# Decoder kernel: places of the rotary, of the first projection, of a norm step and of the gates' transposes in the order of an attention loop

## The chip, the cores and the metric

One core of a Trainium2 chip runs the whole kernel in one launch. The metric is the device time of one execution in microseconds (us); lower is better. An execution is compared with others of the same kernel by its median over several runs.

## What is computed

Two decoder layers on `x` (32 batch rows of 100 tokens, width 256) with a context of 32 x 361 x 192. Each layer adds three parts to x in turn, each on a layer norm of x. Only two of the six parts run the loop that is changed:

- The first part of layer 0: causal self-attention of 16 heads (head width 16), without biases or rotary.
- The third part of layer 0: the same attention with rotary on what makes queries and keys, with biases, then a norm, a gate over 8 experts (softmax, best two) and the sum of the two experts' products, and a second norm.

```python
qkv = x @ w_qkv                                    # first part
scores = jnp.einsum('bhqd,bhkd->bhqk', q, k) / math.sqrt(HD)
scores = jnp.where(causal[None, None], scores, jnp.float32(-1000000000.0))
o = jnp.einsum('bhqk,bhkd->bhqd', jax.nn.softmax(scores, axis=-1), v)
...
q_in = _apply_rope(xh, sin, cos).reshape(B, S, E)  # third part: q and k from q_in, v from x
x1 = _layer_norm(x + attn_out, ln1_w, ln1_b)
gates = jax.nn.softmax(x1 @ gate_w.T + gate_b, axis=-1)
expert_outputs = jnp.einsum('bsd,efd->bsef', x1, expert_w) + expert_b[None, None]
```

All data is float32.

## The kernel before, in words

The six parts run one after the other as stages. x lies in SBUF as eight groups of four batch rows (G = 4, 400 tokens a group). `heads_attention` (from L275) serves the first and the third stage. It is handed functions for what differs: `norm(g, part)`, which makes the normed group g in four parts, `turn`, `res`, which adds the output to x, and `fill(s, part)`, which puts other work into the loop.

The loop (L461) has one step s for each batch row, 32 in all, and in the third stage nine more in which only fill works. It is written as a pipeline: in step s the scores of row s + 1 are made and masked, the weights of row s are transposed and summed with its values, and row s - 1 is divided and projected out. With i = s mod 4, the steps of a group also project queries and keys of the next group (m = 0 at i = 0, m = 1 at i = 1, both halves of the keys at i = 2) and norm the group after that. The order in which the code issues instructions is the order in which PE, DVE, ACT and POOL each run theirs (`in_order`): an instruction that waits holds up all behind it on its engine. Across engines, semaphores order what depends on each other.

The names that the text uses:

- `queries_or_keys(g, m)` (L289): two products into one PSUM tile, then copies. For m = 0, 1 there are two copies, one for even and one for odd heads. In the first stage ACT makes one (L309) and DVE the other (L311); in the third ACT makes both (L305). The keys are copied by ACT (L313, L315).
- `scores` (L348) writes two PSUM tiles sc, `masked` (L363) adds the mask on DVE, `lowered` (L372) takes the row maximum on DVE (L376) and subtracts it on POOL (L377), `exponentials` (L379) is on ACT (L382). Each is done in two halves of eight heads.
- `turn_weights` (L385): four times four transposes of exponentials on PE (L389) with a copy eT on ACT each (L394). The first two take the first half of the heads, the last two the second half.
- `values` (L327), `sums` (L398, with the copy `back` on ACT, L410), `divided` (L414: four transposes on PE, then reciprocal and product on DVE, L423 and L425), `turn_sums` (L428, copy oT on ACT, L437), `output` (L441).
- The tiles called mm share four PSUM banks between all of these; a new tile waits until the copy that empties its bank's last tile is done.
- In the first stage `norm` part 1 takes statistics (on DVE, with one power on POOL, L174), part 2 subtracts and scales on DVE (L183); parts 0 and 3 do nothing. `turn` transposes the group and copies it to xT (L210, L131, L133); it stays at the head of step i = 0.
- In the third stage `norm` part 0 takes statistics, part 1 scales on ACT (L192), part 2 transposes (L945), and part 3 makes the rotary xrT with four DVE instructions (L956, L958 twice, L961). `turn` only hands over.
- The third stage's `fill` (L1111 on): `gated` makes `xg`, expert inputs times gate, on DVE (L1061), in part 0 for the step's second expert and in part 3 for the next step's first; `experts` multiplies on PE in parts 1 and 2 (L1073) and adds to `acc` on DVE (L1079), from step 9 on. A table says at which 4 * i + part a group's `rows_of` (bias and norm after attention), `gating` (transposes of x1, product with the gate weights, softmax, best two) and `gates_turned` come, one group behind the attention.

Quoted from the loop before:

```python
if g < NG:
    if i == 0:
        turned_[g] = turn(g)
    for m in ((0,), (1,), (2, 3), ())[i]:
        queries_or_keys(g, m)
if i >= 1 and g + 1 < NG:
    norm(g + 1, i - 1)
```

Of the kernel before, what the change touches and what calls it, by code (L numbers as in the profile page):

```python
# [22 lines left out]
NG = B // G  # L23
# [43 lines left out]
def kernel(ctx: ExitStack, tc: tile.TileContext, io: dict, out: bass.AP):  # L67
# [19 lines left out]
    def sc_tile():  # L87
        return psum["sc"][1].tile([P, 2, 512], F32, tag="sc", name="sc")

    def mm_tile():  # L90
        return psum["mm"][1].tile([P, 512], F32, tag="mm", name="mm")
# [18 lines left out]
    def row(name, n=T):  # L110
        a, b = ROW_AT[name]
        return rows[:n, a:b]

    def col(name, i=0, n=P):
        a, _ = COL_AT[name]
        return cols[:n, a + i : a + i + 1]
# [10 lines left out]
    def evac(dst, src):  # L127

        turn[0] += 1
        if turn[0] % 2:  # L130
            nc.vector.tensor_copy(dst, src)  # L131
        else:
            nc.scalar.copy(dst, src)  # L133
# [67 lines left out]
    def transposed(dst, src, gain=None, bias=None, tiles=None):  # L201

        if tiles is None:
            ps = sc_tile()
            ps = [ps[:, 0, :], ps[:, 1, :]]
        else:
            ps = [tiles() for _ in range(2)]
        for c in range(2):
            for i in range(G):
                nc.tensor.transpose(  # L210
                    ps[c][:, i * T : (i + 1) * T], src[:, i, c * P : (c + 1) * P], ident[:T, :T]
                )
        for c in range(2):
            if gain is None:
                evac(dst[:, c, :], ps[c][:, :GT])
            else:
                evac_affine(dst[:, c, :], ps[c][:, :GT], col(gain, c), col(bias, c))
# [7 lines left out]
    def in_order(more=mybir.EngineType.Pool):  # L225

        e = mybir.EngineType
        return tc.manual_schedule(engines={e.PE, e.DVE, e.Activation, more})
# [46 lines left out]
    def heads_attention(pool, w, wo, bias, norm, turn, res, fill):  # L275
# [103 lines left out]
        def exponentials(s, hf):  # L379

            ex = pool.tile([T, 8, T], F32, tag="ex", name="ex", bufs=4)
            nc.scalar.activation(ex, sms.pop((s, hf)), AF.Exp, scale=0.25)  # L382
            exs[s, hf] = ex
# [63 lines left out]
        with in_order():  # L447
            for part in range(4):
                norm(0, part)
            turned_[0] = turn(0)  # L450
            for m in range(4):
                queries_or_keys(0, m)
            values(0)
            ps = scores(0)
            for hf in range(2):
                masked(0, hf, ps[hf])
                lowered(0, hf)
                exponentials(0, hf)
            for part in range(4):
                norm(1, part)  # L460
            for s in range(B + 1 + fill.steps):  # L461
                g, i = s // G + 1, s % G
                more = s + 1 < B
                if more:
                    ps = scores(s + 1)
                    masked(s + 1, 0, ps[0])
                if g < NG:
                    if i == 0:
                        turned_[g] = turn(g)
                    for m in ((0,), (1,), (2, 3), ())[i]:  # L470
                        queries_or_keys(g, m)
                if i >= 1 and g + 1 < NG:
                    norm(g + 1, i - 1)
                fill(s, 0)
                if 1 <= s <= B:
                    divided(s - 1)
                if more:
                    lowered(s + 1, 0)
                    masked(s + 1, 1, ps[1])
                if i == 3 and g + 1 < NG:  # L480
                    norm(g + 1, 3)
                if s < B:
                    turn_weights(s)
                fill(s, 1)
                if more:
                    lowered(s + 1, 1)
                    values(s + 1)
                if 1 <= s <= B:
                    turn_sums(s - 1)
                if more:  # L490
                    exponentials(s + 1, 0)
                if s < B:
                    sums(s)
                fill(s, 2)
                if 1 <= s <= B:
                    output(s - 1)
                if more:
                    exponentials(s + 1, 1)
                fill(s, 3)


# [10 lines left out]
    with tc.tile_pool(name="a0", bufs=2) as pool:  # L512
        xns = {}

        def norm(g, part):
            if part == 1:
                xns[g] = stats(xs[g], G, tag="n")
            elif part == 2:
                xn = pool.tile([T, G, D], F32, tag="xn", name="xn")
                centered(xn, xs[g], G, xns[g])  # L520
                xns[g] = xn
# [10 lines left out]
        def fill(s, part):  # L532
            pass
# [16 lines left out]
    with tc.tile_pool(name="x0", bufs=2) as pool, tc.tile_pool(name="x0p", bufs=1) as fixed:  # L550
# [288 lines left out]
        with in_order():  # L839
# [11 lines left out]
            for n in range(-4, B + 1):  # L851
# [14 lines left out]
                g = (n + 4) // G + 1  # L866
                if (n + 4) % G == 3 and g < NG:
                    lnTs[g] = latents_turned(lns.pop(g))
                g = (n + 5) // G
# [55 lines left out]
    with tc.tile_pool(name="f0", bufs=2) as pool:  # L925
# [44 lines left out]
        x1s, x1Ts, wts, accs = {}, {}, {}, {}  # L970

        parts = {}
# [15 lines left out]
        def gating(g, part):  # L988
            if part == 0:
                x1T = pool.tile([P, 2, GT], F32, tag="x1T", name="x1T")  # L990
                transposed(x1T, x1s.pop(g), "f0_ln1w", "f0_ln1b", tiles=mm_tile)

                pg = mm_tile()
                project(
                    pg[:, :GT], [f0_wg[:, c, :] for c in range(2)],
                    [x1T[:, c, :] for c in range(2)],
                )
                lgT = small.tile([E, GT], F32, tag="wtT", name="lgT", bufs=2)
                nc.scalar.activation(lgT, pg[:E, :GT], AF.Identity, bias=col("f0_gb", 0, E))
                x1Ts[g], parts[g] = x1T, lgT  # L1000
                return
            if part == 1:
                lgT = parts[g]
                pg = mm_tile()
                for i in range(G):
                    nc.tensor.transpose(
                        pg[:T, i * E : (i + 1) * E], lgT[:, i * T : (i + 1) * T], ident[:E, :E]
                    )
                lg = small.tile([T, G, E], F32, tag="lg", name="lg")
                p3 = pg[:T, : G * E].rearrange("p (g e) -> p g e", e=E)  # L1010
                nmx = small.tile([T, G], F32, tag="nmg", name="nmg")
                nc.vector.tensor_reduce(nmx, p3, AX.X, ALU.max, negate=True)
                nc.vector.tensor_tensor(lg, p3, bc(nmx, 2, E), ALU.add)
                nc.scalar.activation(lg, lg, AF.Exp)
                parts[g] = lg
                return
            lg = parts.pop(g)
            sm = small.tile([T, G], F32, tag="smg", name="smg")
            nc.vector.tensor_reduce(sm, lg, AX.X, ALU.add)
            nc.vector.reciprocal(sm, sm)  # L1020
            gt = small.tile([T, G, E], F32, tag="gt", name="gt")
            nc.vector.tensor_tensor(gt, lg, bc(sm, 2, E), ALU.mult)
            _, hot = top2(pool, gt, G, row("iota", P))
            wt = small.tile([T, G, E], F32, tag="wt", name="wt")
            nc.vector.tensor_tensor(wt, hot[:T, 0], hot[:T, 1], ALU.add)
            nc.vector.tensor_tensor(wt, wt, gt, ALU.mult)
            wts[g] = [wt]
# [83 lines left out]
        def fill(s, part):  # L1111

            g, i = s // G, s % G


            n = 2 * (s - 2 * G - 1)
            if part % 3 == 0:
                upto = n + part // 3 + 1
                if s >= B:
                    upto += 2  # L1120
                if s < B + G:
                    upto = min(upto, E * (NG - 1) - 1)
                while done[0] <= min(upto, loads[0] - 1):
                    gated(done[0])
                    done[0] += 1
                    gates()
            if 1 <= g <= NG:
                for at, f, *args in (
                    (3, rows_of, 0), (4, rows_of, 1), (6, rows_of, 2), (9, gating, 0),
                    (10, gating, 1), (11, gating, 2), (14, gates_turned),  # L1130
                ):
                    if 4 * i + part == at:
                        f(g - 1, *args)
                        if at == 14:
                            stored[0] = E * g
                            gates()
            if 3 <= g and i == 1 and part in (0, 1, 3):
                end(g - 3, part)
            if part in (1, 2) and 0 <= n < E * NG:
                experts(n // E, n % E // 2, part - 1)  # L1140
# [33 lines left out]
    with tc.tile_pool(name="a1", bufs=2) as pool, tc.tile_pool(name="a1p", bufs=1) as fixed:  # L1174
# [242 lines left out]
        with in_order():  # L1417
            for part in range(11):
                project_group(0, part)
            for n in range(16 * NG + 12):  # L1420
                g, at = n // 16, n % 16
# [501 lines left out]
    with tc.tile_pool(name="f1s", bufs=2, side="right") as pool, in_order(SP):  # L1923
# [134 lines left out]
        for n in range(len(units) + 2):  # L2058
            if n < len(units):
                h, m = units[n]  # L2060
# [243 lines left out]
```

## Time and profile before

| what | value |
|---|---|
| median of 3 runs (lowest, highest) | 3555.65 us (3551.82, 3564.07) |
| the profiled execution: time, span | 3556.24 us, 3554.4 us |
| mean granted TensorE clock | 0.975 |
| PE busy, share of the span | 3353.6 us, 94% |
| DVE, ACT, POOL busy | 1873.7 us (53%), 1602.8 us (45%), 1258.7 us (35%) |
| first stage's loop | about 36 to 282 us of the span |
| third stage's loop, with its start and tail | about 767 to 1345 us of the span |

PE is TensorE's matmul, PEld its weight load, DVE VectorE, ACT ScalarE, POOL GpSimd, SP SyncE. L12 is line 12 of the kernel. In the view of stages, each line is a stretch of the span (start:end in us), then its length, then busy us and instructions of each engine, the granted PE clock as a share of full speed, the busy share of DMA, and GB/s. In the view of waits, a line is: engine, what waited, `<-` who released it and with what, us in total, times, the longest. In the view in order of time, a line is: start, duration, engine, source line, operation, output `<-` inputs, sizes, count, and in brackets the idle time before it with its releaser. Several equal instructions in a row are merged, so a duration with x8 is that of all eight.

### The profile page before, as it was taken

The numbers are of one execution on the slowest core, as the hardware profiler recorded it, in microseconds if no ns is written. First come the engines' busy times: TensorE is split into PE (matmuls) and PEld (weight loads), VectorE is DVE, ScalarE is ACT, GpSimd is POOL, SyncE is SP. The second block draws the span as 40 slices with busy tenths as digits, with TensorE's granted clock in tenths as the row PEclk, the third lists the DMA queues.
The fourth block names the chain that finished last, engine by engine and source line by source line (L and its number), as shares of the span: only waits on it lengthen the run. The fifth ranks groups of instructions, "written<-read, shape, count | busy, mean of one in ns | idle before, by whom it ended". The sixth has DMA issues, their size and how long they took to land. (4 is left out here: it accounts for less than half of the span.)

```text
span 3554.4 us, 66360 instructions
## 1 busy us (share of the span) xinstructions
PE 3353.6 (94%) x25978; PEld 2256.7 (63%) x25978; DVE 1873.7 (53%) x5328; ACT 1602.8 (45%) x3533; POOL 1258.7 (35%) x917
## 2 busy tenths in 40 slices
PE   7998999978989987999999999999999999999997
PEld 5775666646556643333466666666666668899997
DVE  6777777747676755755456464554646542011111
ACT  4664666646444414567454454545444442211111
POOL 3445887744444421000233333333233332012221
PEclk9999999989999998999999999999999999999999
DMA  2002000000101111000100000000000003466665
GB/s 84 2 2 64 23 26 23 16 17 9 28 22 31 27 38 47 1 1 1 41 14 19 19 25 21 20 26 19 20 27 18 25 13 111 140 178 184 187 179 146
DMA packets 109218, 168.15 MB, mean 47 GB/s; under 512 B 14996, under 2 KB 89628, under 8 KB 108444
## 3 DMA queue, kind: packets, MB, share of 16 engines
q1 hardware_dynamic: 94238, 145.60, 13.5%
q0 software_dynamic: 12688, 15.36, 2.4%
q8 instruction: 207, 3.39, 0.4%
q10 hardware_dynamic: 1982, 2.95, 0.2%
q14 instruction: 103, 0.84, 0.1%
HBM read 138.32 MB, written 28.82 MB: 47 GB/s over the span
## 5 line engine op out<-in xcount | busy, mean ns | idle before, releaser
L1696 POOL TENSOR_TENSOR ex<-ex,rc 100x1444 f32<-100x1444 f32 x128 | 332.1, 2594 | 785.1 <-DVE rc L1695 743.4
L1687 ACT ACTIVATE ex<-s,nmx 100x361 f32<-100x361 f32 x512 | 303.1, 594 | 143.4 <-DVE nmx L1678 143.4
L377 POOL TENSOR_TENSOR s<-s,nmx 100x800 f32<-100x800 f32 x128 | 210.1, 1641 | 332.4 <-DVE nmx L376 251.1
L1294 ACT ACTIVATE h<-sc,cols 128x800 f32<-128x800 f32 x256 | 222.4, 924 | 134.1 <-PE sc L1288 133.7
L1678 DVE CUSTOM_DVE_ANT_0 s<-sc,mb 100x361 f32<-100x361 f32 x512 | 250.5, 527 | 7.6 <-PE sc L1671 7.6
L2151 POOL DMA_INDIRECT acc_dram<-y,xg x57 | 89.0, 1562 | 451.1 <-DVE y L2150 243.0
L2133 ACT ACTIVATE hgT<-sc 128x1024 f32<-128x1024 f32 x57 | 58.4, 1024 | 351.2 <-PE sc L223 344.8
L1073 PE MATMUL mm<-xg,f_we 128*128 128x400 f32 x512 | 195.2, 527 | 19.3 <-ACT back L410 11.2
L223 PE MATMUL sc<-xgT,w1b 128*128 128x128 f32 x1824 | 213.1, 275 | 0.4 <-DMA w1b<-in_f_w 0.4
L2150 DVE TENSOR_SCALAR y<-mm,gx 128x256 f32<-128x256 f32 x57 | 27.6, 484 | 348.1 <-PE mm L223 348.1
L223 PEld LDWEIGHTS sc<-xgT,w1b 128*128 128x128 f32 x1824 | 208.2, 192 | 0.7 <-issue 0.6
L223 PE MATMUL mm<-wx,hgT 128*128 x912 | 206.1, 379 | 0.0
L1671 PE MATMUL sc<-kT,qT 64*100 64x361 f32 x1024 | 197.6, 463 | 0.0
L1643 PE MATMUL mm<-x_wa,cT 128*128 128x512 f32 (+1 forms) x512 | 191.1, 496 | 0.1
L1703 PE MATMUL mm<-ident,ex 100*128 100x100 f32 (+1 forms) x1536 | 168.0, 257 | 18.7 <-ACT kT L1625 9.7
L223 PEld LDWEIGHTS mm<-wx,hgT 128*128 128x128 f32 x912 | 169.0, 190 | 20.6
L1721 PEld LDWEIGHTS mm<-eT,vb 128*64 128x64 f32 (+1 forms) x3072 | 136.7, 137 | 67.4 <-issue 66.2
L1613 PE MATMUL mm<-cT,x_wa 128*128 128x361 f32 x512 | 178.1, 471 | 0.7 <-DVE lnT L148 0.7
L174 POOL TENSOR_TENSOR rs<-va,neghalf 100x4 f32<-100x4 f32 (+1 forms) x96 | 95.4, 997 | 216.9 <-DVE va L170 120.4
L1703 PEld LDWEIGHTS mm<-ident,ex 100*128 100x128 f32 (+1 forms) x1536 | 142.6, 151 | 39.8 <-ACT kT L1625 14.0
L1710 ACT COPY eT<-mm 128x400 f32<-128x400 f32 (+1 forms) x256 | 125.7, 491 | 89.2 <-PE mm L1703 87.7
L1721 PE MATMUL mm<-eT,vb 128*64 128x100 f32 (+1 forms) x3072 | 162.3, 254 | 0.0
(346 smaller groups left out, 7221.6 us busy)
## 6 DMA issues: line engine op xcount, KB each, us to landing
w1b<-in_f_w SPq DMA_DIRECT2D x57, 1024.0 KB
wb<-wt_dram SPq DMA_DIRECT2D x64, 200.0 KB
wx<-in_f_w SPq DMA_DIRECT2D x8, 1024.0 KB
xg<-sorted_dram SPq DMA_DIRECT2D x57, 132.5 KB
cb<-in_ctx SPq DMA_DIRECT2D x32, 192.0 KB
cT<-in_ctxT SPq DMA_DIRECT2D x32, 180.5 KB
cT<-in_ctxT SPq DMA_DIRECT2D x64, 90.2 KB
x<-in_x SPq DMA_DIRECT2D x8, 400.0 KB
```

Of the source, the lines that this page charges most:

```text
L223: nc.tensor.matmul(ps, lhsT[k], rhs[k], start=(k == 0), stop=(k == n - 1))
L377: nc.gpsimd.tensor_tensor(sm, sm, bc(nmx, 2, T), ALU.add)
L1073: nc.tensor.matmul(ps[:, :GT], f0_we[:, k, e * D + m * P : e * D + (m + 1) * P], xgs[E * g + e][:, k, :], start=(i > 0 and e == 2 * i and ...
L1294: nc.scalar.activation(h1, both[r2][:, :, :GT], AF.Tanh, bias=col("a1_b1", o))
L1613: nc.tensor.matmul(kTs[u][c][:, :S2], x1_wa[:, m * P : (m + 1) * P], cT[:, 0, :], start=True, stop=False,)
L1643: nc.tensor.matmul(ps[e][:kn, :n], cT[:, 0, at], x1_wa[:, 1024 + c0 : 1024 + c0 + n], start=True, stop=False,)
L1671: nc.tensor.matmul(ps[:T, e, :S2], qT[p0 : p0 + 64, m, tok], kT[p0 : p0 + 64, c, :], start=True, stop=True,)
L1678: nc.vector.tensor_tensor_reduce(s[:, e, :], ps[:T, e, :S2], mb, 1.0, 3.4e38, ALU.add, ALU.min, nmx[:, e : e + 1],)
L1687: nc.scalar.activation(ex[:, 2 * c + e, :], s[:, e, :], AF.Exp, bias=nmx[:, e : e + 1], scale=-1.0, accum_out=sm[:, 2 * c + e : 2 * c + e ...
L1696: nc.gpsimd.tensor_tensor(ex, ex, bc(rc, 2, S2), ALU.mult)
L1703: nc.tensor.transpose(pt[:kn, j * T : (j + 1) * T], ex[:, j, k0 : k0 + kn], ident[:T, :T])
L1721: nc.tensor.matmul(po[64 * e : 64 * e + 64, m * T : (m + 1) * T], vb[k][:kn, v0 + 64 * h : v0 + 64 * h + 64] if k < 2 else vb[2 + u % 2][: ...
```

## The change

Five moves in the order of the code; no instruction is added or taken out, and no tile gets another size.

1. `queries_or_keys(g, 0)` at i = 0 is issued behind `turn_weights` and fill part 1, instead of right behind `turn`.
2. `norm(g + 1, 1)` at i = 2 is issued at that same place, instead of before `divided`.
3. `norm(g + 1, 3)` at i = 3 is issued at the end of the step, before fill part 3, instead of before `turn_weights`.
4. `gating` gets a fourth part: its transposes are a part of their own.
5. In fill's table the transposes go from place 9 to place 8 (i = 2, part 0, before `divided`); the gates' product stays at 9, and the two parts after it keep 10 and 11.

```diff
@@ heads_attention, the loop
                 if g < NG:
                     if i == 0:
                         turned_[g] = turn(g)
-                    for m in ((0,), (1,), (2, 3), ())[i]:
+                    for m in ((), (1,), (2, 3), ())[i]:
                         queries_or_keys(g, m)
-                if i >= 1 and g + 1 < NG:
+                if i in (1, 3) and g + 1 < NG:
                     norm(g + 1, i - 1)
                 fill(s, 0)
                 if 1 <= s <= B:
@@
                 if more:
                     lowered(s + 1, 0)
                     masked(s + 1, 1, ps[1])
-                if i == 3 and g + 1 < NG:
-                    norm(g + 1, 3)
                 if s < B:
                     turn_weights(s)
                 fill(s, 1)
+                if i == 0 and g < NG:
+                    queries_or_keys(g, 0)
+                if i == 2 and g + 1 < NG:
+                    norm(g + 1, 1)
                 if more:
                     lowered(s + 1, 1)
                     values(s + 1)
@@
                     output(s - 1)
                 if more:
                     exponentials(s + 1, 1)
+                if i == 3 and g + 1 < NG:
+                    norm(g + 1, 3)
                 fill(s, 3)
@@ gating
             if part == 0:
                 x1T = pool.tile([P, 2, GT], F32, tag="x1T", name="x1T")
                 transposed(x1T, x1s.pop(g), "f0_ln1w", "f0_ln1b", tiles=mm_tile)
+                x1Ts[g] = x1T
+                return
+            if part == 1:
+                x1T = x1Ts[g]
 
                 pg = mm_tile()
@@
-                x1Ts[g], parts[g] = x1T, lgT
+                parts[g] = lgT
                 return
-            if part == 1:
+            if part == 2:
                 lgT = parts[g]
@@ fill
-                    (3, rows_of, 0), (4, rows_of, 1), (6, rows_of, 2), (9, gating, 0),
-                    (10, gating, 1), (11, gating, 2), (14, gates_turned),
+                    (3, rows_of, 0), (4, rows_of, 1), (6, rows_of, 2), (8, gating, 0),
+                    (9, gating, 1), (10, gating, 2), (11, gating, 3), (14, gates_turned),
```

## The prediction

> **Reading order and what bounds the kernel.** I read the shares of the span first (PE 94% busy, DVE 53%, ACT 45%, POOL 35%), then busy time by stage, then who PE waits for in the two stages that the change touches, then the order of time of single steps there. "Step s" is one turn of the loop at L461, i = s mod 4; W1 to W4 are the four groups of `turn_weights`, D is `divided`, Q the projection of m = 0, X0 and X1 the expert products of fill parts 1 and 2.
>
> ```profile
> core 0: us, PE busy (x) PEld busy (x) DVE busy (x) ACT busy (x) POOL busy (x), PEclk, DMA share, GB/s
> 36.00:282.00 246.00, 233.25 (x3098) 173.14 (x3096) 182.34 (x331) 157.57 (x319) 104.22 (x131) 1.00 0.01 2
> 847.00:1267.00 420.00, 378.70 (x3225) 250.34 (x3224) 291.97 (x662) 179.97 (x358) 175.25 (x160) 0.98 0.11 28
> ```
> Only these stages run the edited loop (with the start, 767 to 847). The first leaves PE 13 us idle in 246, at full clock; the second 41 us in 420, and not always at full clock. In both PE sets the end, so an edit is worth the PE waits that it removes, less those that it makes. PE's waits from 847 to 1267:
>
> ```profile
> PE mm L1073 <- ACT back L410: 11.2, 4, 2.8
> PE mm L1073 <- DVE xg L1061: 8.1, 7, 1.9
> PE mm L210 <- ACT eT L394: 5.8, 5, 1.2
> PE mm L223 <- DVE x1T L148: 2.6, 4, 1.1
> PE mm L223 <- ACT x1T L139: 2.2, 3, 0.8
> ```
> The first and third to fifth are what the change aims at. How the first arises, in time (s = 15, i = 3):
>
> ```profile
> 993.04 4.07 POOL L377 TENSOR_TENSOR s<-s,nmx 100x800 f32<-100x800 f32 x1 [10.48 <-DVE nmx L376]
> 995.76 2.19 DVE L961 TENSOR_TENSOR xrT<-xrT,xwT 128x800 f32<-128x800 f32 x1
> 997.14 0.87 ACT L382 ACTIVATE ex<-s 100x800 f32<-100x800 f32 x1 [2.63 <-POOL s L377]
> 997.91 0.47 ACT L410 COPY back<-mm 128x400 f32<-128x400 f32 x1
> 998.44 5.70 PE L1073 MATMUL mm<-xg,f_we 128*128 128x400 f32 x8 [2.81 <-ACT back L410]
> ```
> POOL's `lowered` takes 4.07 us here and 1.52 elsewhere; the rotary's last add takes 2.19 instead of 0.98. They run at once and hold each other up. The exponential, the copy `back` behind it on ACT, and X1 (whose PSUM bank `back` frees) come late by that. X1 then takes 5.70 us instead of 2.95: PE fell to half clock.
>
> **Sum, first attention** (s = 0 to 31). No instruction is added anywhere; no DMA moves but the loads `wb`, which follow `xg` on SP.
>
> Q moved behind W: PE waits 0.88 us for `xT` between transposes and Q, six times in the trace (5.3 us), and W3 0.23 us for the bank that the qT copy frees. Now D and W1 (1.0 us of PE) cover the copies. W2 takes the bank of the first copy (done about 2.6 us after the scores start; W2 gets there at 2.8), so I see no new wait. On DVE the qT copy (0.64 us) now lies between the second mask and the second maximum; the weights need that result only in the next step, with some 2 us to spare. 6 x (0.88 + 0.23) = **-6.7 us**.
>
> `norm(g+1, 1)` at i = 2, here statistics on DVE (146.12 to 148.54, 2.4 us), moved behind the second mask:
>
> ```profile
> 148.47 0.26 DVE L423 RECIPROCAL rc<-mm 100x16 f32<-100x16 f32 x1
> 151.01 0.99 DVE L376 TENSOR_REDUCE nmx<-s 100x8 f32<-100x800 f32 x1
> 152.14 1.52 POOL L377 TENSOR_TENSOR s<-s,nmx 100x800 f32<-100x800 f32 x1 [0.40 <-DVE nmx L376]
> 153.69 0.88 ACT L382 ACTIVATE ex<-s 100x800 f32<-100x800 f32 x1 [0.67 <-POOL s L377]
> 154.06 1.70 PE L389 MATMUL mm<-ident,ex 100*100 100x100 f32 x16
> ```
> Where the statistics stand before, they are free: the reciprocal waits for D anyway, which PE ends at 148.4 behind two projections. Behind the second mask (ends 150.97) they push the second maximum to 153.3, its POOL add to 154.4 (the power of 1.02 us goes ahead of it on POOL, and is done by then), the exponential to 156.0 to 156.9. W3 of the next step reads it, and is due at 154.75: half of 1.70 us after 154.06, just after the exponential's present end at 154.57. So PE waits about 2.2 us, with W4, values, sums and output queued behind. ACT's four copies eT stand behind the same exponential, but W4 needs the first only at 157.4. Six groups: **+13.2 us**. Bounds: 0, if D came 2.4 us earlier (nothing moves it), and 2.4 each.
>
> Does such a hole also cost clock? The Trainium skill, page "TensorE: Matmul & The Clock Gate", section "Why this matters for your kernels", puts the limit at PE-idle gaps over about 3 us, a whole window of idle: 2.2 us would cost nothing. Stretches of 3.4 us of this trace say otherwise:
>
> ```profile
> 847.00:850.40 3.40, 1.50 (x33) 0.98 (x35) 3.23 (x12) 0.57 (x2) 1.78 (x5) 1.00 0.00 0
> 850.40:853.80 3.40, 3.40 (x44) 2.16 (x36) 2.48 (x4) 1.86 (x4) 3.00 (x3) 0.50 0.02 5
> ...
> 905.00:908.40 3.40, 2.17 (x22) 1.72 (x20) 2.34 (x5) 3.40 (x9) 1.52 (x1) 1.00 0.15 50
> 908.40:911.80 3.40, 2.65 (x8) 1.63 (x9) 0.67 (x1) 1.28 (x3) 0.00 (x0) 1.00 0.00 0
> ```
> PE busy 1.50 of 3.40 us (one gap of 1.90) gives half clock for the next 3.4; 2.17 does not. Of all such stretches in these stages none with over 55% busy is followed by half clock. So I take the trace: a gap of 2.0 us, of which 1.6 must fall in one stretch, trips in about two of three phases. Half clock for 3.4 us loses up to 1.7, I take 1.5: 4 x 1.5 = **+6 us** (by the rule 0; at most 6 x 1.7 = 10). The same page, section "Part 4: PE-mode transpose", says that transposes don't count as PE-busy in the same way. By that the new run of 28 transposes (xn, D, W, some 3 us) in front of Q would trip the clock at every i = 0: 6 x 1.7 = 10 us more. But the stretch at 905.00 holds transposes alone and keeps its clock; I count nothing.
>
> First stage: -6.7 + 13.2 + 6 = **+12.5 us**.
>
> **Sum, third stage.** Rotary (`norm(g+1, 3)`, 0.98 + 1.05 + 0.98 = 3.0 us of DVE uncontended) at the end of i = 3: POOL's add is back to 1.52 us and the exponential comes at 994.6. In the new order X1 also takes the bank of `turn_sums`, free since 994.5. X1 then follows the gates' product at 995.6. Gone: 4 x 2.81 = 11.2 us, and the half clock that the trace shows from 932.3, 997.2 and 1065.5 (3.4 + 6.8 + 3.4 us, half of it lost, 6.8). I take **-17 us**; bounds 11 and 18.
>
> Price, at i = 0 behind it (s = 12, 16, 20, 24): DVE starts the rotary only after `res` (0.5 us after the scores start), then come `xg`, the mask, the second `xg`. The first `xg` lands at 4.4, the second at 6.2; X0 is ready for them at 3.0 and 5.8, since Q no longer runs ahead of it. PE waits 1.4 + 0.4, with Q, values, sums and X1 behind, and saves 0.4 of old waits: 4 x 1.45 = +5.8, and about 1.2 for a clock that trips now and then: **+7 us**; bounds 0 and 13.
>
> Steps 0, 4, 8 have no experts: Q waits for the rotary (2.0, 1.6) or `back` (1.25), then W3 for Q's copies (1.8, 1.45), with a half-clock stretch at 836.8. Q behind W meets the rotary nearly done (it ends 3.4 us after the scores start; Q is due at 3.0): 1.7 + 4.6 + 2.2 = **-8.5 us**.
>
> i = 2: the scaling on ACT (2.06 us) stands before the copies eT, so PE waits 1.16; now it follows them. The transposes of x1, now ahead of D, have D and W (2.1 us) to cover `x1T` before the gates' product; x1 is ready (scaled by 1032.4, read at 1037.5). Four groups with experts: 7.2. Where no experts run, the scaling stands before oT and the output product waits for it: s = 2 nothing, s = 6 0.7. s = 26 and 30: 1.6. **-9.5 us**. The tail after s = 32 has nothing between the two pieces: 0.
>
> Third stage: -17 + 7 - 8.5 - 9.5 = **-28 us**.
>
> **Total.** -28 + 12.5 = -15.5. The profiled execution took 3556.24 us (span 3554.4), 0.6 above the median 3555.65: 3556.2 - 15.5, about 3541.
>
> **Rivals.**
> A, slower: DVE's moved blocks trip the clock each time, for two stretches as at 997.2. Place: W3 at i = 3 of the first attention (six) and X0 at i = 0 of the third stage (four). Price 3.4 each. Without trips the sums are -28 - 1.2 + 6.5 = -22.7; ten at 3.4 make it +11, 3567. It decides from 3.3 us a hole on. For: 6.8 us at half clock did follow one hole. Against: two of the other three took one stretch, one none. 0.13.
> B, no change: the third stage's cover fails in part: X1 finds its wait again (gates' product in X0's bank, waiting for `acc`), half of the 17 stays; about -7, 3549. Against: with the rotary gone `acc` follows the mask at once. 0.26.
> C, the first attention loses nothing, as exp and W3 have slack that this trace hides, and no clock trips: -6.7 - 28, 3521. Against: the slack at W3 reads 0.1 us. 0.09.
> Forecast: 0.52.
>
> **Numbers.** 0.3% (10.7 us) is about what a measurement can tell from no change. The forecast's own spread (3530 to 3550) lies partly within 0.3%. Faster 0.58, same 0.28, slower 0.14. Range 3524 to 3560: C's edge to B's and a bit of A.
>
> **What would show it.** Right: POOL L377 1.5 us throughout the third stage; no L1073 wait for `back`; a new wait of L389 for ACT ex of about 2 us, six times, in the first attention, with half-clock stretches there; L1073 waiting for `xg` 1.4 us at i = 0; the L210 wait for eT gone. The first stage longer by 6 to 17 us, the third shorter by 20 to 33. Wrong: the first attention not longer, or a third stage whose steps i = 0 grow by over 4 us each.

## The result, and the profile after

The changed kernel takes 3536.49 us (median of 6 runs, 3531.97 to 3541.01), against 3556.76 for the kernel before (6 runs): a ratio of 0.9938, interval 0.9927 to 0.995. The forecast was 3541. The profiled execution after took 3532.22 us with a span of 3530.5, at a mean granted clock of 0.977.

The two stages, in the columns used above. Each stretch ends where its loop now ends, so that both hold the same work as before:

```profile
core 0: us, PE busy (x) PEld busy (x) DVE busy (x) ACT busy (x) POOL busy (x), PEclk, DMA share, GB/s
36.00:292.00 256.00, 237.77 (x3085) 177.89 (x3084) 183.15 (x331) 155.62 (x316) 102.72 (x131) 0.96 0.01 2
848.00:1243.00 395.00, 371.99 (x3224) 247.21 (x3225) 286.57 (x661) 180.18 (x357) 162.06 (x158) 1.00 0.12 30
```

The first attention became longer and lost clock (1.00 before, 0.96 now). The third stage became shorter: PE is idle 23 us of it instead of 41, and half clock is down from 17.1 us to one stretch of 3.4 us (from 850.4). PE's waits from 848 to 1243:

```profile
PE mm L1081 <- DVE xg L1069: 13.7, 11, 1.9
PE mm L431 <- DVE o L425: 3.7, 3, 1.9
PE mm L389 <- DVE o L425: 1.6, 1, 1.6
PE mm L389 <- ACT x1T L139: 1.6, 1, 1.6
```

L1081 is the experts' product, L1073 before. Its wait for `back` (11.2 us) is gone, and so is that of the transposes at L210 for eT (5.8). Its wait for `xg` grew from 8.1 to 13.7. From 36 to 282, in the first attention, two waits are left:

```profile
PE mm L389 <- ACT ex L382: 12.2, 6, 2.5
PE mm L389 <- DVE qT L311: 2.1, 7, 0.7
```

The first of them is new: six times, as the six groups have it. Gone is the projection's wait for xT, which the same view of the kernel before has:

```profile
PE mm L223 <- DVE xT L131: 5.3, 6, 0.9
```

The steps place the difference. Their lengths are read from one start of `scores` to the next, before and after:

| steps | before, us | after, us | sum of the differences |
|---|---|---|---|
| first attention, i = 0 (s = 4 to 24) | 9.54, the last 9.35 | 8.03 | -8.9 |
| first attention, i = 3 (s = 3 to 23) | 6.28, the last 6.54 | 9.60, 9.59, 8.02, 9.53, 9.63, 10.07 | +18.5 |
| third stage, s = 0, 4, 8 | 10.39, 12.39, 10.12 | 7.55, 8.38, 7.98 | -9.0 |
| third stage, i = 3 (s = 11, 15, 19, 23) | 18.58, 19.76, 18.47, 17.00 | 14.12 each | -17.3 |
| third stage, i = 0 (s = 12, 16, 20, 24) | 13.00 | 14.67 | +6.7 |
| third stage, i = 2 (s = 2 to 26) | 9.94, 13.53, 18.76, 18.41, 18.76, 18.41, 17.13 | 9.66, 12.33, 16.40, 16.28, 16.33, 16.28, 16.33 | -11.3 |

The first attention's loop ends 9.3 us later in relation to its start, the third stage's loop takes 30.6 us less, and the stages between them, which the change does not touch, took 2.4 us less. Their time is 511 to 516 us from one kernel of this study to the next. PE is idle 24.1 us of them both before and after; half clock covers 30.7 us before and 23.9 after.

Where the third stage gained, at s = 15, i = 3, in order of time:

```profile
982.54 1.52 POOL L377 TENSOR_TENSOR s<-s,nmx 100x800 f32<-100x800 f32 x1 [10.47 <-DVE nmx L376]
984.10 0.87 ACT L382 ACTIVATE ex<-s 100x800 f32<-100x800 f32 x1
984.88 0.47 ACT L410 COPY back<-mm 128x400 f32<-128x400 f32 x1
985.07 2.95 PE L1081 MATMUL mm<-xg,f_we 128*128 128x400 f32 x8
```

POOL's add takes 1.52 us instead of 4.07, the exponential follows it, `back` follows that, and X1 starts with no wait (no bracket) and at full clock (2.95 us, not 5.70). The rotary has moved to the start of the next step, where X0 waits for the DVE work behind it:

```profile
991.25 0.99 DVE L965 TENSOR_TENSOR xrT<-xrT,xwT 128x800 f32<-128x800 f32 x1
992.16 0.98 DVE L1069 TENSOR_TENSOR xg<-x1T,wb 128x800 f32<-128x800 f32 x1
993.29 3.32 PE L1081 MATMUL mm<-xg,f_we 128*128 128x400 f32 x8 [1.40 <-DVE xg L1069]
```

Where the first attention lost, at s = 15, i = 3:

```profile
156.63 0.18 DVE L162 BATCH_NORM_AGGREGATE mv<-st 100x2 f32<-100x6 f32 x1
156.93 0.98 DVE L376 TENSOR_REDUCE nmx<-s 100x8 f32<-100x800 f32 x1
158.09 1.52 POOL L377 TENSOR_TENSOR s<-s,nmx 100x800 f32<-100x800 f32 x1
159.64 0.87 ACT L382 ACTIVATE ex<-s 100x800 f32<-100x800 f32 x1 [2.91 <-POOL s L377]
160.57 1.29 PE L389 MATMUL mm<-ident,ex 100*100 100x100 f32 x8 [1.95 <-ACT ex L382]
```

The row maximum follows the last of the statistics, then POOL's add, the exponential and W3, each directly behind the one before. W3 waits 1.95 us for it, and its eight transposes then take 1.29 us, against 0.93 behind the hole at s = 11, because the clock has dropped (0.50 from 160.94, shown below).

### The profile page after: what moved, and what is told of

It is laid out like the page before. It is cut to its first block, busy times and chain, and to the rows that moved or that the text cites. A ratio compares the mean times of both kernels' runs of the same rounds, so it can differ in the third digit from the quotient of the medians.

```text
span 3530.5 us, 66384 instructions
## 1 busy us (share of the span) xinstructions
PE 3347.5 (95%) x25978; PEld 2258.8 (64%) x25978; DVE 1869.2 (53%) x5328; ACT 1603.5 (45%) x3533; POOL 1243.4 (35%) x917
## 3 DMA queue, kind: packets, MB, share of 16 engines
q1 hardware_dynamic: 94238, 145.60, 13.7%
q10 hardware_dynamic: 1982, 2.95, 0.2%
## 5 line engine op out<-in xcount | busy, mean ns | idle before, releaser
L377 POOL TENSOR_TENSOR s<-s,nmx 100x800 f32<-100x800 f32 x128 | 195.0, 1523 | 338.9 <-DVE nmx L376 220.9
L1081 PE MATMUL mm<-xg,f_we 128*128 128x400 f32 x512 | 191.4, 517 | 14.2 <-DVE xg L1069 13.7
```

The costliest lines, as they stand in the source:

```text
L377: nc.gpsimd.tensor_tensor(sm, sm, bc(nmx, 2, T), ALU.add)
L1081: nc.tensor.matmul(ps[:, :GT], f0_we[:, k, e * D + m * P : e * D + (m + 1) * P], xgs[E * g + e][:, k, :], start=(i > 0 and e == 2 * i and ...
```

## The experiments

Every ratio is to the kernel before, with a 95% interval. "From before" or "from after" says which kernel was edited.

### Each move alone

`q_only`, from before: the first move alone.

```diff
-                    for m in ((0,), (1,), (2, 3), ())[i]:
+                    for m in ((), (1,), (2, 3), ())[i]:
...
+                if i == 0 and g < NG:
+                    queries_or_keys(g, 0)
```

> The kernel before with only the first projection (m = 0) moved behind the weights' transposes. Theory of the prediction (a wait removed is worth its length, at the place where it stood): first attention -1.5 us at each i = 0, six times, -9; third stage, where the rotary stays at its old place and is done in time: s = 4 about -4, s = 8 about -2.5, s = 0 about -2, s = 12 to 24 about -0.4 each. In all -19 us, about 3538, most of what the whole change gives. Rival (the moves add up on their own, each with its share of -20): no more than -9 -8 in the two stages as in the whole change, and the other moves must then bring the rest of the third stage's -30 alone.

3557.09 us (10 runs), ratio 1.000, 0.999 to 1.001: no gain. The first attention gains 5.8 us (i = 0: 9.54 to 8.60), s = 0 gains 2.9. But s = 4 goes from 12.39 to 12.99 and s = 8 from 10.12 to 12.06. Around s = 4:

```profile
814.51 4.00 POOL L377 TENSOR_TENSOR s<-s,nmx 100x800 f32<-100x800 f32 x1 [4.66 <-ACT eT L394]
817.16 2.19 DVE L963 TENSOR_TENSOR xrT<-xrT,xwT 128x800 f32<-128x800 f32 x1
819.85 0.85 PE L418 MATMUL mm<-ident,back 128*100 128x128 f32 x4 [1.91 <-ACT back L410]
```

With the projection out of the way, D is next, and it waits for `back`, which the same collision of POOL's add with the rotary has made late. One wait stood behind the other. That is the smaller part of the loss: some of the later steps were longer by half-clock stretches at other places than before (s = 6, 10, 18, 23: 16.58, 20.45, 20.15, 20.03). PE's idle and busy times, under `q_rotary`, split the two.

`norm1_only`, from before: the second move alone.

```diff
-                if i >= 1 and g + 1 < NG:
+                if i in (1, 3) and g + 1 < NG:
...
+                if i == 2 and g + 1 < NG:
+                    norm(g + 1, 1)
```

> The kernel before with only norm part 1 at i = 2 moved behind the weights' transposes, in both stages. Theory: the first attention's statistics make PE wait 2 us for the exponential at i = 3, six times, and half clock follows in five of six: +18 us there; the third stage's scaling behind the eT copies takes 1.2 us off each i = 2 with gating: -5. In all +13, about 3570. Rival (the hole at i = 3 needs the earlier Q and is not there alone): about -5, 3552.

3567.16 us (7 runs), ratio 1.0028, 1.0015 to 1.004: slower. The first attention is 12.5 us longer, by 13.5 us at i = 3 (8.03, 8.02, 8.02, 9.52, 8.02, 9.85). Two of the six holes tripped the clock here (half clock followed), five of six in the changed kernel.

`rotary_only`, from before: the third move alone.

```diff
-                if i == 3 and g + 1 < NG:
-                    norm(g + 1, 3)
                 if s < B:
                     turn_weights(s)
...
+                if i == 3 and g + 1 < NG:
+                    norm(g + 1, 3)
                 fill(s, 3)
```

> The kernel before with only the rotary at the end of step i = 3; Q stays ahead of the weights. Theory: POOL L377 is back at 1.52 us and X1's wait of 2.81 us with its half clock goes (-17), but Q now waits about 2.5 us for the rotary at every i = 0, with all of PE behind it and half clock in some: +10 to +16 at s = 12 to 24, +2.5 at s = 4 and 8. In all about 0, 3557 (3552 to 3562). Rival (each move brings its share alone): -17 + 7 = -10, 3547.

3559.16 us (10 runs), ratio 1.001, 1.0 to 1.0019. Steps 11, 15, 19, 23 fall to 14.12 as in the changed kernel. Steps 12, 16, 20, 24 grow from 13.00 to 18.19, 16.89, 15.69, 15.69 and give most of it back, since the projection still stands ahead of the weights; half clock at s = 10 and 18 (21.81 and 20.44 us) gives back the rest. PE's waits in the third stage begin:

```profile
PE mm L223 <- DVE xrT L961: 13.1, 5, 2.6
```

`gating_only`, from before: moves four and five (the part split as in the change's diff, and the table).

```diff
-                    (3, rows_of, 0), (4, rows_of, 1), (6, rows_of, 2), (9, gating, 0),
-                    (10, gating, 1), (11, gating, 2), (14, gates_turned),
+                    (3, rows_of, 0), (4, rows_of, 1), (6, rows_of, 2), (8, gating, 0),
+                    (9, gating, 1), (10, gating, 2), (11, gating, 3), (14, gates_turned),
```

> The kernel before with only the gates' transposes and product split and the transposes at place 8. Theory: the scaling still stands on ACT ahead of the copies, so the x1T copy on ACT comes late, and the third transposed group of weights waits for its bank: only about 0.5 us of 1.97 is saved at each i = 2: -4, about 3553. Rival (the split alone removes the wait of the gates' product and the 1.16 us): -10, 3547.

3548.27 us (10 runs), ratio 0.9974, 0.9965 to 0.9984: nearer to the rival's figure. Steps 10, 14, 18, 22 fall to 17.57 and 17.56, s = 6 to 12.62.

So the four edits alone give about +1, +11, +3 and -8 us, together +7. In one kernel they give -20. They are no separate gains.

### Which moves belong together

`q_rotary`, from before: moves one and three, as above.

> The kernel before with two of the moves, the first projection (m = 0) behind the weights and the rotary at the end of step i = 3; the norm step and the gates stay. Alone they gave +1.0 and +3.1 us. Theory (each alone leaves or makes the wait that the other removes: with Q late but the rotary at its old place, `divided` waits for `back`; with the rotary late but Q early, Q waits for the rotary): together -9 in the first attention (no holes there), and in the third stage -2.9 - 4 - 2.1 at steps 0, 4, 8, -17 at i = 3 and +7 at i = 0: -28, about 3528. Rival (the moves add up, and the third stage's gain is due to the gates and the norm step): +4, 3560.

3536.48 us (4 runs), ratio 0.9946, 0.993 to 0.9963: 20 us, where 28 were expected. Each of the two alone gives nothing. Steps 0, 4, 8, 11, 12, 15 and their like have the lengths of the changed kernel to within 0.01 us. The first move takes the projection out of the rotary's way at i = 0, and the third takes the rotary out of POOL's way at i = 3; each uncovers what the other removes.

Waits are not all of it. From the start of step 1 to that of step 30 of the third stage, in the columns of the stages, for the kernel before, `q_only`, `rotary_only` and `q_rotary`:

```profile
805.03:1222.04 417.01, 377.77 (x3430) 254.05 (x3427) 297.03 (x660) 194.10 (x384) 179.85 (x169) 0.98 0.10 24
792.53:1220.39 427.86, 389.17 (x3431) 259.73 (x3427) 298.45 (x661) 194.28 (x385) 181.46 (x172) 0.95 0.09 23
801.29:1219.98 418.69, 380.89 (x3431) 256.54 (x3427) 291.03 (x660) 194.94 (x385) 164.48 (x169) 0.97 0.10 23
792.96:1197.03 404.07, 375.28 (x3431) 251.47 (x3427) 291.74 (x661) 194.31 (x385) 166.13 (x172) 0.99 0.09 24
```

PE's idle time, length less PE busy, is 39.2 us before, 38.7 and 37.8 with one move alone, and 28.8 with both: the pair takes 10.5 us of waits away, the two alone 2.0 together. PE's busy time for the same work is 11.4 and 3.1 us longer with one move alone, and 2.5 shorter with both; half clock covers 20.5, 44.4, 27.3 and 10.2 us of these loops. So of the 25 us by which the pair beats the sum of the two in this stage, some 8.5 are waits and some 17 clock. That half clock would grow so much with the first move alone was not forecast.

The pair takes as long as the whole change (3536.48, 3536.49): the other three edits add nothing in sum. By the profiles they cost 14.9 us in the first attention (its loop at +9.3 against -5.6) and bring 14.9 in the third stage (-30.6 against -15.8).

### The first attention's hole

`stats_back`, from after: the second move undone in the first attention only, where no biases are given.

```diff
+                if i == 2 and g + 1 < NG and bias is None:
+                    norm(g + 1, 1)
...
-                if i == 2 and g + 1 < NG:
+                if i == 2 and g + 1 < NG and bias is not None:
                     norm(g + 1, 1)
```

> The changed kernel, but in the first attention norm part 1 (the statistics) stands at its old place ahead of `divided`; in the third stage it stays moved. Theory: the six holes of 1.95 us before the third group of weights and their half clock go: the first attention ends 18 us earlier, and the rest stays: 3518, ratio 0.989 to the kernel before. Rival (the holes only moved work within a stage that has slack, or the exponential is late for another reason): no change from 3536.

3518.93 us (4 runs), ratio 0.9897, 0.9882 to 0.9911. Steps i = 3 are back at 6.27, PE waits 0.7 us for ex, as in the kernel before, and no stretch behind step 0 has half clock. Steps i = 0 take 8.61, not 8.03: with no hole ahead of them, W3 waits 0.37 us for the half of xT that ACT copies, behind an exponential (s = 12):

```profile
127.54 0.87 ACT L382 ACTIVATE ex<-s 100x800 f32<-100x800 f32 x1 [0.67 <-POOL s L377]
128.32 0.47 ACT L133 COPY xT<-mm 128x400 f32<-128x400 f32 x1
128.84 0.89 PE L389 MATMUL mm<-ident,ex 100*100 100x100 f32 x8 [0.37 <-ACT xT L133]
```

`hole_filled`, from after: in the first attention at i = 3, the transposes of W2, the group ahead of the hole, are done four times more. These 16 transposes a step are needless; the last pass writes the same values.

```diff
-                for j in range(4):
+                again = 5 if bias is None and s % G == 3 and s < B - 2 * G and r == 1 else 1
+                for j in [j for _ in range(again) for j in range(4)]:
```

> The changed kernel with the second group's four transposes done four times more in the first attention's steps i = 3 (s = 3 to 23), so that 16 needless transposes run in the hole; results are the same. PE is busy, the wait ends when it did. Theory (half clock comes when PE is busy under some 55% of a stretch of 3.4 us, and transposes count as busy): five half-clock stretches go, step i = 3 takes 8.0 us instead of 9.6: -7.5, about 3529. Rival by the page's rules (transposes do not count as busy; or the half clock has another cause than the hole): half clock stays, 3536, or later by what transposes at half clock add.

3528.05 us (6 runs), ratio 0.9925, 0.9911 to 0.9938. That interval overlaps the one of the changed kernel (0.9927 to 0.995), so the medians alone do not settle it; the steps do. Steps i = 3 take 8.17 to 8.19, five of six, where those that tripped took 9.53 to 9.63: with added work they are shorter. The hole costs what it did, but not the clock. The stretches of the changed kernel, first one that did not trip (from 126.81), then one that did (from 157.53) with the stretch behind it:

```profile
126.81:130.23 3.42, 1.84 (x14) 1.54 (x14) 3.38 (x9) 2.45 (x5) 0.72 (x3) 1.00 0.00 0
157.53:160.94 3.41, 1.46 (x16) 1.22 (x14) 3.41 (x8) 1.30 (x3) 2.17 (x4) 1.00 0.00 0
160.94:164.36 3.42, 3.42 (x29) 2.58 (x30) 3.23 (x5) 2.06 (x6) 1.52 (x1) 0.50 0.02 5
```

And the same hole filled:

```profile
155.80:159.20 3.40, 2.82 (x33) 2.62 (x30) 3.40 (x7) 1.05 (x2) 2.41 (x4) 1.00 0.00 0
159.20:162.60 3.40, 3.40 (x49) 2.58 (x49) 3.33 (x6) 2.06 (x7) 1.52 (x1) 1.00 0.00 0
```

What PE did from 155.80 to 159.20 is almost all transposes (of D and of W), and the clock stays at 1.00. The traces list them as MATMUL, and one of 100 columns follows another at 0.085 us, where expert products of 400 columns follow at 0.335: the same time per column. One stretch of this kernel still tripped, at s = 23, with PE busy 46% of the stretch ahead of it; that step took 11.79 us.

### The collision of POOL and DVE

`rotary_twice`, from after: at the old place of the rotary, for s = 11, 15, 19, 23, its four DVE operations once more, into a tile that nobody reads.

```diff
+                if i == 3 and g + 1 < NG and bias is not None and s > 2 * G:
+                    norm(g + 1, 4)
                 if s < B:
                     turn_weights(s)
...
+            if part == 4:
...
+                nc.vector.tensor_tensor(w4, l4, bc(bc(rope[:, 0], 1, G), 1, 2), ALU.mult)
+                for c in range(2):
+                    nc.vector.tensor_tensor(
+                        w4[:, c], l4[:, 1 - c], bc(rope[:, 1 + c], 1, G), ALU.mult
+                    )
+                nc.vector.tensor_tensor(xwT, xwT, xlT, ALU.add)
```

> The changed kernel with a needless second rotary (four DVE instructions of the same shapes and kinds into a scratch tile, nothing uses them) at the old place, ahead of `turn_weights` at i = 3, for s = 11, 15, 19, 23. Theory (DVE and POOL hold each other up there, and `acc` on DVE comes late behind it): POOL L377 takes 4 us again, the last scratch add 2.2, and PE waits some 2.8 us ahead of the gates' product or X1 in each of the four, with half clock in most: +15, about 3551. Rival (only the PSUM bank that X1 took was at fault, and that is another one now): POOL slow, but PE as in the changed kernel, 3537.

3545.44 us (8 runs), ratio 0.9966, 0.9954 to 0.9977: the wait comes back, in part. At s = 15:

```profile
990.36 3.10 POOL L377 TENSOR_TENSOR s<-s,nmx 100x800 f32<-100x800 f32 x1 [10.48 <-DVE nmx L376]
991.09 0.98 DVE L972 TENSOR_TENSOR xwT<-xlT,rope 128x800 f32<-128x800 f32 x1
992.11 2.27 DVE L974 TENSOR_TENSOR xwT<-xlT,rope 128x400 f32<-128x400 f32 x2
994.79 2.95 PE L1093 MATMUL mm<-xg,f_we 128*128 128x400 f32 x8 [1.84 <-ACT back L410]
```

POOL's add takes 3.10 us where it takes 1.52 without the extra rotary, and X1 waits 1.84 us for `back`, four times (7.4 us in all). In the kernel before it was 4.07 and 2.81: there the two half products ran at 1.05 us and the last add at 2.19, here the half products take 2.27 and the last add 0.99. So DVE and POOL hold each other up at one of these operations or another. Why it is that one was not tried. Steps 11, 15, 23 take 16.03 instead of 14.12, and s = 19, with one half-clock stretch, 17.70.

### A cheaper place for the rotary, and the best version

`rot_behind_xg`, from after: for s = 12, 16, 20, 24 the rotary and the turn are issued at i = 0 behind fill part 0, so behind `xg`.

```diff
-                    if i == 0:
+                    if i == 0 and not (bias is not None and s > 2 * G):
                         turned_[g] = turn(g)
...
                 fill(s, 0)
+                if i == 0 and g < NG and bias is not None and s > 2 * G:
+                    norm(g, 3)
+                    turned_[g] = turn(g)
...
-                if i == 3 and g + 1 < NG:
+                if i == 3 and g + 1 < NG and not (bias is not None and s > 2 * G):
                     norm(g + 1, 3)
```

> The changed kernel, but the rotary for the steps i = 0 with experts (s = 12, 16, 20, 24) is issued in that step, behind fill part 0 and its expert input, ahead of `divided`; elsewhere it stays at the end of i = 3. Theory: X0 no longer waits 1.4 + 0.4 us for its inputs; Q, 0.6 us late for the rotary, waits that much: step i = 0 takes about 13.3 us instead of 14.67, four times: -5.5, about 3531. Rival (a later rotary delays `divided`, the second mask and POOL's add, and the wait comes back at Q, the weights or the sums): same or slower, 3536 to 3545.

3529.07 us (5 runs), ratio 0.9926, 0.9913 to 0.9938. The four steps fall from 14.67 to 13.87, 3.2 us in all, somewhat over half of what was expected. PE's waits:

```profile
PE mm L1084 <- DVE xg L1072: 8.1, 7, 1.9
PE mm L431 <- DVE o L425: 3.9, 3, 1.9
PE mm L223 <- DVE xrT L968: 2.1, 5, 0.5
```

X0 no longer waits (8.1 us, as in the kernel before), and its eight products take 2.95 us instead of 3.32. But in each of the four steps the projection now waits 0.40 us for the rotary (the 0.5 is s = 8, as in the changed kernel), and `sums` waits 0.41 us behind it: of 1.40 + 0.37 some 0.8 come back, which leaves 1.0, near to the 0.80 that a step fell by. The medians (3536.49 and 3529.07) lie 7.4 us apart, but the intervals overlap; the profiled executions lie 3.7 apart (3532.22 and 3528.55), with 17.1 us of half clock in the first attention in both.

`both`, from after: `stats_back` and `rot_behind_xg` together.

> The two edits of the kernels stats_back and rot_behind_xg together on the changed kernel. Theory: they lie in different stages and add up: -18 - 5.5, about 3512.5, ratio 0.9875 to the kernel before. Rival: as in the two alone.

3514.91 us (4 runs), ratio 0.9883, 0.9868 to 0.9897: the best version of this study, some 40 us under the kernel before (3555.30 beside it) and, by the ratios, some 20 under the changed one. Its interval overlaps that of `stats_back`, so the 4 us between those two are not settled by the medians; the steps show them (13.87 against 14.68).

## Why the prediction was right

Its total was near (3541 for 3536.49), and its large terms were right in sign, place and about in size. Some of the nearness is chance: between the two profiled executions lie 24.0 us, against the forecast's 15.5, and 2.4 of them in stages that the change does not touch.

- **X1's wait at i = 3 of the third stage.** Forecast -17, measured -17.3, by the mechanism named: POOL's add back at 1.52 us, no wait for `back`, no half clock. `rotary_twice` brings the wait back with the collision.
- **Its price at i = 0.** Forecast +7 in two terms: +5.8 for waits and +1.2 for clock. (The waits as written, 1.4 + 0.4 - 0.4, make 1.4 a step and not 1.45.) Measured +6.7, all of it without clock: the gap of X0 is the 1.40 us forecast, the second `xg` makes the fifth product 0.3 us late, and no stretch there trips.
- **Steps 0, 4, 8.** Forecast -1.7, -4.6, -2.2; measured -2.84, -4.01, -2.14. The sum holds (-8.5, -9.0).
- **i = 2 of the third stage.** Forecast -9.5, measured -11.3, since the steps give a little more than their waits: at s = 10 to 22 waits of 1.65 to 1.97 us go, as forecast (1.8), and the steps are 2.1 to 2.4 shorter. s = 2 gives 0.3 where nothing was forecast.
- **First attention, Q.** Forecast 6 x 1.11 = -6.7. `stats_back`, which has no hole, gives 0.93 a step (9.54 to 8.61). The step that failed is "I see no new wait": it looked at W2 and the copy on DVE, and W3 waits 0.37 us for the bank that the copy of xT on ACT frees. In the changed kernel that wait is hidden by the hole ahead of it, and the steps give 1.51 each, -8.9.
- **First attention, the hole.** Forecast +13.2 for waits and +6 for clock, 19.2; measured 18.5 at i = 3. The split was off in both terms. The gaps are 1.95 us (the last 2.45), not 2.2, and five of six tripped, not four. The step that did not trip grew by 1.75, those that did by 3.25 to 3.53: six times 1.75 (10.5), five times some 1.6 (8.0).
- **The clock rule.** By the rule quoted from the Trainium skill (page "TensorE: Matmul & The Clock Gate", section "Why this matters for your kernels") the holes would have cost no clock. The trace of after has five half-clock stretches behind gaps of 1.95 to 2.45 us. By the page's statement on transposes (section "Part 4: PE-mode transpose") the prediction would have had the clock drop at every i = 0 of the first attention; no stretch there trips, and `hole_filled` holds the clock with almost nothing but transposes. Whether they count in full is not shown, nor whether these are transposes in the mode that the page means. The prediction's own limit, 55% busy, held in the trace that it was read from and not in later ones:

```profile
867.92:871.33 3.41, 2.04 (x18) 1.43 (x18) 3.38 (x8) 1.45 (x3) 1.61 (x3) 1.00 0.04 9
871.33:874.74 3.41, 3.41 (x10) 2.04 (x9) 2.28 (x3) 1.10 (x4) 2.47 (x2) 0.50 0.64 170
941.01:944.42 3.41, 1.56 (x5) 0.98 (x6) 3.07 (x4) 1.63 (x3) 1.04 (x2) 1.00 0.02 4
944.42:947.84 3.42, 3.42 (x42) 2.22 (x41) 1.70 (x3) 0.87 (x1) 1.08 (x3) 1.00 0.18 60
```

In `q_only` (first two lines) a stretch with PE busy 60%, all of it transposes, is followed by half clock; in `norm1_only` (last two) one with 46%, all of it expert products behind a gap of 2.81 us, is not. So busy time alone does not decide; what PE does in it may count too, which no run here took apart.

- **The rivals.** A asked for clock trips of two stretches at each of ten holes; there were five, of one stretch each, and none at i = 0 of the third stage. B asked for a wait left at X1; there is none. C asked for no hole in the first attention; it is there.

What it did not say is that the moves do not add up one by one. It took the whole change at once, and so the sum came out. The expectation for `q_only` took the Q term out of that sum, and failed by 19 us: 3538 expected, 3557 measured.

Why five of six holes trip in the changed kernel and two of six in `norm1_only` can be read from the traces. The half-clock stretches of the changed kernel's first attention begin at 61.96, 96.09, 160.94, 195.08 and 229.21 us, whole multiples of 3.413 us apart: they lie on a fixed grid, and the holes fall at different places of it. The seven holes that had at least 1.95 us within one stretch of the grid tripped; the five that had 1.64 or less did not.

What stays open: how the clock weighs different work of PE, and why half clock covers 20.5 us of the stages between the loops in one kernel and 34.1 in another.

## What to carry to other kernels

When a wait is removed, look for what becomes due next, and cost the moves that uncover each other as one: here two moves worth nothing alone are worth 20 us together, in part by waits and in larger part by where the clock dropped. A shared loop needs each edit costed in each stage that runs it: the statistics' new place cost the first attention about 15 us, as `stats_back` shows, and a condition on the stage took that back. A hole of 2 us in PE cost almost as much again in clock (some 1.6 us), where it lay badly, so fill it or close it before looking for shorter instructions.

## What the runs showed of the hardware

- Granted clock: a stretch of 3.41 us with PE busy 1.46 us (43%), one gap of 1.95 us in it, was followed by half clock for 3.4 us; one with 1.84 (54%) was not. Whether a hole trips depends on how it lies in these stretches, which stand on a grid of 3.413 us: the same gap of 1.95 us did both. PE's busy share does not decide alone: 60% of transposes was followed by half clock (`q_only`), 46% of expert products was not (`norm1_only`).
- Sixteen needless transposes ahead of a hole made its step shorter (9.53 to 9.63 us without them, 8.17 to 8.19 with them), because PE was busy 2.82 of 3.40 us there and the clock stayed at 1.00.
- A POOL add of row maxima (100x8) to a 100x800 float32 tile in SBUF took 1.52 us by itself, 3.10 and 4.07 us beside DVE operations on two tiles of 128 rows; those took 2.27 instead of 1.05 and 2.19 instead of 0.99. One of DVE's operations in each such group stayed at 0.98, although POOL was at work.
